# Attention times FFN on one core: sums spread through DRAM, weights transposed on TensorE, another order beside the output products

## The chip, the cores and the metric

The kernel runs on one core of a Trainium2 chip. The metric is device time in microseconds (us) of one execution, the median of several. The engines are TensorE (PE, with its weight loads as PEld), VectorE (DVE), ScalarE (ACT), GpSimd (POOL) and SyncE (SP, which here only issues DMAs). Each engine runs its own instructions in the order in which the program gives them, and waits on semaphores for the others.

## The reference

The input x has 4 batches of 512 rows of 512 floats. Attention and a quantised FFN work on the same normalised x and are multiplied:

```python
xn = layernorm(x)
q, k, v = split(xn @ w_qkv)                 # 16 heads of 32
q, k = rope(rmsnorm(q) * q_gamma), rope(rmsnorm(k) * k_gamma)
s = softmax(causal(q @ k.T / sqrt(32))) @ v @ w_out
W = lambda wq, scale: (wq - 128) * scale[:, None]    # wq are int32
g = silu((silu(xn @ W(wq_gate).T) * (xn @ W(wq_up).T)) @ W(wq_down).T)
out = x + s * g
```

Gate and up weights are 1408 x 512, the down weights 512 x 1408, all as int32 with small values. The scales are applied after the products.

## The kernel before

One launch holds everything. The work is cut into 16 units: batch b (0 to 3) by head group g (0 to 3, four heads each). The order is written out by hand (a manual schedule): the program text's order is each engine's order, and there is no planner. Each unit is a hidden window followed by an attention window.

**The hidden window** (`hidden_window`, L702) computes FFN hidden tiles f of one chunk (chunks of 2, 3, 3, 3 tiles for g = 0 to 3; a tile is 256 of the gate and up rows). `hidden` (L578) makes the products (L585, x split into a high part xh and a rest xl in two f32r products), `gate` and `gated` (L594, L599) the silu and product. Between them stand fills: the last probabilities of the unit before, its sums, the transposes of the new q and k (`Projection.turn`, L417), in norm windows the transposes of the next batch's x (`Norm.turn`, L342).

**The attention window** comes in three forms. Units (0,0) to (0,2) use `attention_window` (L759): probabilities are transposed on PE (`turn`, L493). Units (0,3) to (3,2) use `placed_window` (L824): DVE transposes 32 x 32 blocks (`blocks`, L511, instruction L521), and four DMAs on SP place them (`spread`, L523). Unit (3,3) uses `last_window`. In each, step t (0 to 3) takes query tile t: `scores` (L445), `probabilities` (L462; DVE masks and takes the row's minimum at L473, ACT exponentiates at L483 and sums the row), `values` (L536). Beside them run the next unit's qkv projection: `product` (L366, PE), `square` (L379: ACT squares q and k, then copies v out, L381 and L382) and `rotate` (L384: DVE L402, L405, L409; POOL L410, L316, L317, L412), and the down products `contract` (L624, L632).

Three special places: in **norm windows** (b,3) with b below 3, `Norm.cut` (L349) splits the next batch's xnT, with a copy on ACT and a subtraction L353 on the engine named (two on POOL, two on DVE in placed windows). In **g = 0 windows** of batches 1 to 3, `beside(t)` runs `Result.project` (L673, products L678) and `finish` (L686) of the batch before. In others it does nothing.

**Sums.** ACT leaves the row sums of the softmax, one column per head and tile. `spread_sums` (L547) takes reciprocals on DVE (L553) and repeats each over 32 columns on POOL (L554). `turn_sums` (L559) transposes that on PE (four transposes, L563), ACT copies the result to rT (L564), and `divide` (L566) multiplies the values' bank by rT on DVE.

**Weights.** The FFN weights are prepared once, during batch 0. 34 tiles are loaded as int32 (22 of gate and up with four 128 x 128 blocks each, 12 of down with 4, 4 or 3). `turn_weights` (L250) casts a tile to bf16 on ACT (L256) and starts a transposing DMA on SP (L258); `finish_weights` (L261) subtracts 128 on DVE into the final f32r place and collects the largest value (L265). The prologue (L967) does the first four; then `weights()` (L278) runs after each f of a hidden window and each t of an attention window in batch 0, until all are done:

```python
        for _ in range(n):
            if turning and now[0] - turning[0][0] >= 2:
                finish_weights()
        load_weights(n)
```

**PSUM.** There are four pools: ps_a with four banks (scores, qkv, hidden and output products), ps_t with two (`bank_t`, L104: all transposes, some qkv products), and one each for the values and for the down products.

Of the kernel before, what the change touches and what calls it, by code (L numbers as in the profile page):

```python
# [21 lines left out]
P = 128  # L22
# [29 lines left out]
def interleaved(  # L52
# [40 lines left out]
    ps_t = ctx.enter_context(tc.tile_pool(name="ps_t", bufs=2, space=PSUM))  # L93
    ps_v = ctx.enter_context(tc.tile_pool(name="ps_v", bufs=1, space=PSUM))
    ps_d = ctx.enter_context(tc.tile_pool(name="ps_d", bufs=1, space=PSUM))
    ctx.enter_context(tc.manual_schedule())

    def work(name):
# [86 lines left out]
    def load_scales():  # L185
# [5 lines left out]
            at += n  # L191
        return srow, at

    sdown = const.tile([P, D], F32, name="sdown")

    def prepare_scales(srow, at):
        tp = bank_t("sps")
# [32 lines left out]
    todo = list(preparations())  # L230
    n_prep = len(todo)
    largest = const.tile([P, n_prep], F32, name="largest")
    loaded, turning, finished = [], [], set()

# [10 lines left out]
                nc.sync.dma_start(raw.bitcast(U32), src.bitcast(U32))  # L247
                loaded.append((now[0], room, raw, k, dst, name))

    def turn_weights():  # L250


        _, room, raw, k, dst, name = loaded.pop(0)
        halves_ = raw.bitcast(BF16)
        n = k * P
        nc.scalar.copy(halves_[:, :n], raw.bitcast(U32))  # L256
        turned = halves_[:, n:].rearrange("p (c r) -> p c r", r=P)
        nc.sync.dma_start(turned, halves_[:, :n], transpose=True)  # L258
        turning.append((now[0], room, turned, k, dst, name))

    def finish_weights():  # L261

        _, room, turned, k, dst, name = turning.pop(0)
        i = len(finished)
        nc.vector.tensor_scalar(  # L265
            dst,
            turned,
            -ZERO_POINT,
            None,
            ALU.add,  # L270
            ALU.max,
            accum_out=largest[:, i : i + 1],
        )
        if len(finished) >= NC:
            rooms.append(room)
        finished.add(name)

    def weights(n=2):  # L278

        now[0] += 1  # L280
        for _ in range(n):
            if turning and now[0] - turning[0][0] >= 2:
                finish_weights()
        load_weights(n)
        for _ in range(n):
            if loaded and now[0] - loaded[0][0] >= 1:
                turn_weights()

    def find_wide():

# [69 lines left out]
    class Projection:  # L360
# [16 lines left out]
            self.banks[t] = bank  # L377

        def square(self, t):  # L379
            bank = self.banks[t]  # L380
            nc.scalar.activation(squares, bank[:, : 2 * P], AF.Square)  # L381
            nc.scalar.copy(self.v[:, t, :], bank[:, 2 * P :])  # L382

        def rotate(self, t, squared=False):  # L384


            bank = self.banks[t]
            name = f"{self.b}_{self.g}_{t}"
            if not squared:
                self.square(t)  # L390
            qk = qp.tile([P, 2 * P], F32, tag="qk", name=f"qk_{name}")
            qs = tp_.tile([P, 2 * P], F32, tag="qs", name=f"qs_{name}")

            def four(a):
                return a.rearrange("p (i h d) -> p i h d", i=2, d=HD)

            def table(k, cols):
                a = tab[:, t, :, k, cols]
                return a.unsqueeze(2).to_broadcast([P, 2, HPG, a.shape[-1]])

            bank4 = four(bank[:, : 2 * P])
            nc.vector.tensor_tensor(four(qk), bank4, table(0, slice(0, HD)), ALU.mult)  # L402
            for lo, hi in ((0, half), (half, 0)):
                lo, hi = slice(lo, lo + half), slice(hi, hi + half)
                nc.vector.tensor_tensor(  # L405
                    four(qs)[:, :, :, lo], bank4[:, :, :, hi], table(1, lo), ALU.mult
                )
            ss = small.tile([P, 2 * HPG], F32, tag="ss", name=f"ss_{name}")
            nc.vector.tensor_reduce(ss, heads(squares), AX.X, ALU.add)  # L409
            nc.gpsimd.tensor_tensor(qk, qk, qs, ALU.add)  # L410
            inverse_root(ss, ss, HD * RMS_EPS)
            nc.gpsimd.tensor_tensor(  # L412
                heads(qk), heads(qk), ss.unsqueeze(2).to_broadcast([P, 2 * HPG, HD]), ALU.mult
            )
            self.qk[t] = qk
# [15 lines left out]
    class Step:  # L431
# [30 lines left out]
        def probabilities(self, *js):  # L462

            for j in js:
                if self.first is not None:
                    pr = piece(self.first, self.t + 1)[:, j * self.keys : (j + 1) * self.keys]
                else:
                    i = j % self.per
                    if i == 0:
                        self.pieces.append(next_piece("pr"))  # L470
                    pr = self.pieces[-1][:, i * self.keys : (i + 1) * self.keys]
                least = self.least[:, j : j + 1]
                nc.vector.tensor_tensor_reduce(  # L473
                    out=pr,
                    in0=self.banks[j],
                    in1=mask[:, N - self.keys :],
                    scale=float(HD),
                    scalar=3.0e38,
                    op0=ALU.add,
                    op1=ALU.min,  # L480
                    accum_out=least,
                )
                nc.scalar.activation(  # L483
                    pr,
                    pr,
                    AF.Exp,
                    bias=least,
                    scale=-1.0,
                    accum_out=self.sums[:, self.t, j : j + 1],
                )  # L490
                self.probs.append(pr)

# [54 lines left out]
        def spread_sums(self, tiles=range(NT)):  # L547

            n, cols = len(tiles), slice(tiles[0] * P, (tiles[-1] + 1) * P)
            if tiles[0] == 0:  # L550
                self.sums_spread, self.rT = work(f"spread_{self.id}"), work(f"rT_{self.id}")
            sums = self.sums[:, tiles[0] : tiles[0] + n, :]
            nc.vector.reciprocal(sums, sums)  # L553
            nc.gpsimd.tensor_copy(  # L554
                heads(self.sums_spread[:, cols]),
                sums.rearrange("p t j -> p (t j)").unsqueeze(2).to_broadcast([P, n * HPG, HD]),
            )

        def turn_sums(self, tiles=range(NT)):  # L559
            cols = slice(tiles[0] * P, (tiles[-1] + 1) * P)  # L560
# [5 lines left out]
        def divide(self, tiles=range(NT)):  # L566
# [2 lines left out]
                oT[:, self.g, cols], self.pv[:, cols], self.rT[:, cols], ALU.mult  # L569
            )  # L570

    def steps(b, g, v):
        sums = small.tile([P, NT, HPG], F32, tag="sums", name=f"sums_{b}_{g}")
        pv = ps_v.tile([P, N], F32, tag="pv", name=f"pv_{b}_{g}")
        return [Step(b, g, t, v, sums, pv) for t in range(NT)]

# [125 lines left out]
    def hidden_window(b, g, last, fresh, result, norm, beside):  # L702

        placed = last is not None and last.placed
        if result is not None and not placed:
            result.gate(0)

# [5 lines left out]
        def turned(*tiles):  # L715
# [4 lines left out]
        fills = [  # L720
            lambda: drain(0),
            lambda: drain(2),
            lambda: (last.spread_sums(), fresh.turn()) if last is not None else None,
            lambda: turned(0, 1),
            lambda: turned(2),
            lambda: turned(3),
# [1 line left out]
        for i, f in enumerate(chunks[g]):  # L728
# [22 lines left out]
                fresh.turn()  # L751
            if b == 0:
                weights()
        if last is not None:
            last.turn_sums()
            if not placed:
                last.values()
# [66 lines left out]
    def placed_window(b, g, last, s, fresh, norm, result):  # L824

        def halves(engine, *tiles):
            if norm is not None:
                for t in tiles:  # L830
                    norm.cut(t, engine)

        def beside(t):
            if result is not None:
# [8 lines left out]
        def values():  # L843
            for t in range(NT - 1):
                s[t].values()

        load(0)
        s[0].scores()
        s[1].scores(s[0].whole, s[0].keys)
# [4 lines left out]
        adds = contract_two(b, g)  # L854
        s[1].probabilities(0, 1, 2, 3)
        adds[0]()
        if g == 0:
            fresh.rotate(0, squared=True)
        if last.placed:
            last.values()  # L860
        s[2].scores()
        adds[1]()
        if g == 0:
            last.divide()
        s[0].blocks(0, 1, 2, 3)
        s[0].spread()
        s[2].probabilities(0, 1, 2, 3)
        add = contract(b, g, 2)
        s[2].blocks(0, 1, 2, 3)
        s[2].spread()  # L870
        if g:
            fresh.product(0)
            fresh.rotate(0)
        s[1].blocks(0, 1, 2, 3)
        s[1].spread()
        load(1, 2)
        if g == 0:
            add()
        halves(nc.gpsimd, 0, 1)
        for t in range(NT):  # L880
            if t:

                fresh.product(t, other=t == NT - 1 or (g > 0 and t == NT - 2))
                fresh.rotate(t)
            if t == 1 and g:
                add()
                last.divide()
            if t == 1:
                halves(nc.vector, 2, 3)
            beside(t)  # L890
            if t == 1:
                load(3)
# [74 lines left out]
    def prologue():  # L967
# [18 lines left out]
        norm.cut(3, nc.vector)  # L986
        load_weights(3)
        for _ in range(4):
            turn_weights()
        fresh.product(1)  # L990
        fresh.rotate(1)
        for _ in range(4):
            turn_weights()
        for t in range(2, NT):
            fresh.product(t)
            fresh.rotate(t)
            finish_weights()
            finish_weights()
        load_wqkv(slice(1, 2))
        now[0] += 1  # L1000
        prepare_scales(*scales_in)
# [3 lines left out]
    for u, (b, g) in enumerate(units):  # L1005
# [17 lines left out]
                done.store(t)  # L1023
        if (b, g) == (0, NC - 1):
            next(finding)
            nc.sync.dma_start(wout, w_out.rearrange("(c p) m -> p c m", p=P))
        if b == 0 and 2 + g < NC:
            load_wqkv(slice(2 + g, 3 + g))
        if (b, g) == (0, 0):
            nc.sync.dma_start(sdown, s_down.partition_broadcast(P))  # L1030
        if (b, g) == (0, NC - 2):
            finding = find_wide()
            next(finding)
# [485 lines left out]
```

## Time and profile before

| what | before |
|---|---|
| median of 3 executions | 659.25 us (658.75 to 659.99) |
| profiled execution | 656.71 us |
| its span | 654.9 us (1.8 us lie around it) |
| PE busy | 622.2 us, 95% of the span |
| DVE busy | 482.4 us, 74% |
| ACT busy | 346.3 us, 53% |
| POOL busy | 317.0 us, 48% |
| mean granted TensorE clock | 0.992 |
| DMA | 62.63 MB in 65584 packets |

The profiled execution is 2.5 us below the median. Busy shares are averages over very different stages: batch 0 carries the weights, batches 1 to 3 the output products of the batch before. The profile's chain of work follows the last instruction back to what released it; the waits add up idle time by what ended it; the timeline gives start, duration, engine, line and operation of merged instructions, with idle time and releaser in brackets; and the windows view gives busy time and the granted clock in chosen stretches.

### The profile page before, as it was taken

To read this page: it belongs to the slowest core of one execution; us is meant where nothing else is said; L and a number is where in the kernel's file an instruction comes from. 1 tells how busy PE (TensorE), PEld (TensorE's weight loads), DVE (VectorE), ACT (ScalarE), POOL (GpSimd) and SP (SyncE) were. 2 spreads that over 40 slices of the span, in tenths; PEclk is the share of its full clock that TensorE was granted. 3 is DMA by queue.
4 is the path that set the end of the run, shared out by engine and by line. 5 is a ranking of instruction groups with operands and counts; after the bars stand their busy time and mean duration, and the time that the engine had idled before them with its cause. 6 is when DMAs were issued, how large, how long until landed. Compare 5 with 4: busy or idle time off the path is not lost.

```text
span 654.9 us, 11673 instructions
## 1 busy us (share of the span) xinstructions
PE 622.2 (95%) x3906; PEld 413.7 (63%) x3906; DVE 482.4 (74%) x1248; ACT 346.3 (53%) x895; POOL 317.0 (48%) x365
## 2 busy tenths in 40 slices
PE   4989999999988999999998999999997999999995
PEld 3646757667564576758664476767765467676752
DVE  4677776755988479797998369799798657969553
ACT  2666765646473264546755046464756136464560
POOL 3925235352563626544382633637194442727422
PEclk9999999999999999999998999999999899999999
DMA  8594853100433146243323425523233505333401
GB/s 267 144 215 110 185 133 101 66 1 1 98 82 87 59 130 162 66 96 66 79 44 81 121 48 144 137 61 83 65 80 82 145 1 146 82 73 89 130 1 70
DMA packets 65584, 62.63 MB, mean 96 GB/s; under 512 B 22998, under 2 KB 48876, under 8 KB 65516
## 3 DMA queue, kind: packets, MB, share of 16 engines
q1 hardware_dynamic: 64556, 61.38, 37.7%
q8 instruction: 33, 0.54, 0.3%
q10 hardware_dynamic: 960, 0.43, 0.2%
q14 instruction: 35, 0.29, 0.1%
HBM read 21.80 MB, written 4.19 MB: 40 GB/s over the span
## 4 chain that ended last, share of the span: by engine, by line
PE 79%; DVE 12%; ACT 4%; issue 2%; DMA 2%; POOL 0%; DVEq 0%; ACTq 0%
PE h L585 22%; PE qkv L370 21%; PE so L678 9%; PE sc L452 5%; PE dn L632 5%; PE dn L615 5%; PE pv L539 5%; DVE arena L521 3%; PE pt L499 2%; DVE arena L473 2%; PE qkt L422 2%; DVE qs L405 1%; PE rt L563 1%; ACT arena L483 1%; PE xnt L346 1%
## 5 line engine op out<-in xcount | busy, mean ns | idle before, releaser
L370 PE MATMUL qkv<-wqkv,xnT 128*128 128x384 f32 x512 | 172.5, 490 | 2.3 <-DVE least L473 2.3
L483 ACT ACTIVATE arena<-arena,least 128x128 f32<-128x128 f32 (+3 forms) x256 | 140.6, 551 | 63.4 <-DVE least L473 63.2
L370 PEld LDWEIGHTS qkv<-wqkv,xnT 128*128 128x128 f32 x512 | 96.3, 191 | 69.0 <-issue 4.2
L521 DVE STREAM_TRANSPOSE arena<-arena 128x512 f32<-128x512 f32 (+1 forms) x132 | 126.1, 1002 | 0.0
L410 POOL TENSOR_TENSOR qk<-qk,qs 128x256 f32<-128x256 f32 x64 | 48.2, 753 | 156.0 <-DVE qs L405 156.0
L473 DVE CUSTOM_DVE_ANT_0 arena<-sc,mask 128x128 f32<-128x128 f32 (+3 forms) x256 | 109.3, 485 | 15.1 <-PE sc L452 13.8
L604 POOL TENSOR_TENSOR h<-sil,h 128x512 fp32r<-128x512 f32 x44 | 57.9, 1315 | 110.5 <-ACT h L603 110.5
L317 POOL TENSOR_TENSOR ss<-ss,minus_half 128x8 f32<-128x8 f32 x64 | 106.9, 1671 | 5.3
L381 ACT ACTIVATE squares<-qkv 128x256 f32<-128x256 f32 x64 | 24.5, 383 | 122.5 <-PE qkv L370 98.0
L602 DVE SCALAR_TENSOR_TENSOR sil<-h,scales,sil 128x512 f32<-128x512 f32 x44 | 32.7, 743 | 52.6 <-PE h L585 43.7
L678 PE MATMUL so<-wout,oT 128*128 128x512 f32 x128 | 61.9, 625 | 6.6 <-DVE least L473 6.6
L603 ACT CAST h<-sil 128x512 fp32r<-128x512 f32 x44 | 27.3, 620 | 72.3 <-DVE sil L602 72.3
L402 DVE TENSOR_TENSOR qk<-qkv,tab 128x256 f32<-128x256 f32 x64 | 26.4, 412 | 44.7 <-ACT v L382 44.3
L632 PE MATMUL dn<-wdT,h 128*128 128x512 f32 x208 | 59.0, 419 | 0.0
L632 PEld LDWEIGHTS dn<-wdT,h 128*128 128x128 f32 x208 | 36.9, 188 | 25.8 <-issue 16.0
L585 PE MATMUL h<-xh,wuT 128*128 128x512 f32 x176 | 50.0, 406 | 1.7 <-ACT qT L125 1.7
L585 PE MATMUL h<-xh,wgT 128*128 128x512 f32 x176 | 50.0, 406 | 0.7 <-ACT v L382 0.7
L452 PE MATMUL sc<-kT,qT 32*128 32x512 f32 (+3 forms) x512 | 48.8, 467 | 1.4 <-DVE wdT L265 1.4
L585 PE MATMUL h<-xl,wgT 128*128 128x512 f32 x176 | 48.2, 395 | 0.0
L585 PE MATMUL h<-xl,wuT 128*128 128x512 f32 x176 | 48.1, 395 | 0.0
L483 ACT ACTIVATION_READ_ACCUMULATOR arena<-arena,least 128x1 f32 x256 | 47.9, 187 | 0.0
L678 PEld LDWEIGHTS so<-wout,oT 128*128 128x128 f32 x128 | 24.7, 199 | 33.9 <-issue 23.6
(92 smaller groups left out, 920.7 us busy)
## 6 DMA issues: line engine op xcount, KB each, us to landing
arena<-arena SPq DMA_DIRECT2D x48, 256.0 KB, 4.8
arena<-arena SPq DMA_DIRECT2D x48, 192.0 KB, 3.6
arena<-arena SPq DMA_DIRECT2D x48, 128.0 KB, 3.2
x<-in_L_attn_x SPq DMA_DIRECT2D x16, 256.0 KB, 4.3
out<-o SPq DMA_DIRECT2D x15, 256.0 KB, 4.4
wqkv<-in_L_attn_w_qkv SPq DMA_DIRECT2D x16, 192.0 KB, 3.4
arena<-arena SPq DMA_DIRECT2D x48, 64.0 KB, 2.1
xr<-in_L_attn_x SPq DMA_DIRECT2D x12, 256.0 KB, 3.8
```

What stands on the lines that cost most here:

```text
L317: nc.gpsimd.tensor_tensor(dst, dst, minus_half[:, : dst.shape[-1]], ALU.pow)
L370: nc.tensor.matmul(bank.rearrange("p (i d) -> p i d", i=3), lhsT=xnT[:, c, ts(t, P)], rhs=wqkv[:, c, :, self.g, :], start=(c == 0), stop=( ...
L410: nc.gpsimd.tensor_tensor(qk, qk, qs, ALU.add)
L452: nc.tensor.matmul(bank, lhsT=qT[rows, ts(self.t, P)], rhs=kT[rows, : self.keys], start=True, stop=True,)
L473: nc.vector.tensor_tensor_reduce(out=pr, in0=self.banks[j], in1=mask[:, N - self.keys :], scale=float(HD), scalar=3.0e38, op0=ALU.add, op1 ...
L483: nc.scalar.activation(pr, pr, AF.Exp, bias=least, scale=-1.0, accum_out=self.sums[:, self.t, j : j + 1],)
L521: nc.vector.transpose(way[:, :, blocks], probs[:, :, blocks])
L539: nc.tensor.matmul(self.pv[j * HD : (j + 1) * HD, ts(self.t, P)], lhsT=self.v[:, k, ts(j, HD)], rhs=self.turned[j][:, k], start=(k == 0), ...
L585: nc.tensor.matmul(bank, lhsT=w[:, c, ts(f, P)], rhs=a[:, c, :], start=(c == 0 and a is xh), stop=(c == NC - 1 and a is xl),)
L604: nc.gpsimd.tensor_tensor(to[:, 1, :], sil, to[:, 0, :].bitcast(F32), ALU.subtract)
L632: nc.tensor.matmul(bank, lhsT=h[:, i, a, ts(t, P)], rhs=wdT[:, f, :], start=(i == 0 and a == 0), stop=(f == fs[-1] and a == 1),)
L678: nc.tensor.matmul(self.banks[t], lhsT=oT[:, g, ts(t, P)], rhs=wout[:, g, :], start=(g == 0), stop=(g == NC - 1),)
```

## The change

The change has three parts.

1. **Sums.** In the hidden windows of (b,g) with b above 0 and g above 0, but not (3,3) (8 of 16 units, called `far`), the sums of the unit before are no longer repeated on POOL and transposed on PE. `send_sums` takes the reciprocal and one 32 x 32 block transpose on DVE and writes the result to a DRAM tile with four DMAs; `receive_sums`, called in the placed window between the spreads, reads it back with four DMAs that each broadcast a row to 32 partitions. All sums live in one constant tile.
2. **Weights.** The transposing DMAs go. `cast_weights` casts (one step later than before), and `turn_weights` transposes two tiles on PE into one bank of ps_t, with DVE's subtraction reading PSUM. The identity in bf16 lies in the tile of the down scales, whose load moves to unit (0,3).
3. **Order in `placed_window`.** With g = 0 the next unit's first rotation (and v's copy, now apart from the squares) and s0's blocks and spread come after s2's probabilities. In norm windows all cuts come first and all subtractions go to POOL, the last rotation's addition goes to DVE, and s0's blocks come after s2's probabilities.

```diff
-    def turn_weights():
+    def cast_weights():
...
-        halves_ = raw.bitcast(BF16)
-        n = k * P
-        nc.scalar.copy(halves_[:, :n], raw.bitcast(U32))
-        turned = halves_[:, n:].rearrange("p (c r) -> p c r", r=P)
-        nc.sync.dma_start(turned, halves_[:, :n], transpose=True)
...
+        narrow = raw.bitcast(BF16)[:, : k * P]
+        nc.scalar.copy(narrow, raw.bitcast(U32))
+        cast.append((now[0], room, narrow, k, dst, name))
+
+    def turn_weights(n=2):
+        bank = bank_t(f"wt_{len(finished)}").bitcast(BF16)
+        for i in range(n):
+            _, room, narrow, k, dst, name = cast.pop(0)
+            turned = bank[:, i * 4 * P : (i * 4 + k) * P]
+            for c in range(k):
+                nc.tensor.transpose(turned[:, ts(c, P)], narrow[:, ts(c, P)], ident16)
+            at = len(finished)
+            nc.vector.tensor_scalar(
+                dst,
+                turned.rearrange("p (c r) -> p c r", r=P),
...
     def weights(n=2):
         now[0] += 1
-        for _ in range(n):
-            if turning and now[0] - turning[0][0] >= 2:
-                finish_weights()
+        ready = [c for c in cast[:n] if now[0] - c[0] >= 1]
+        if ready:
+            turn_weights(len(ready))
         load_weights(n)
         for _ in range(n):
-            if loaded and now[0] - loaded[0][0] >= 1:
-                turn_weights()
+            if loaded and now[0] - loaded[0][0] >= 2:
+                cast_weights()
...
+        def send_sums(self):
+            sums = self.sums[:, :HPG, :]
+            nc.vector.reciprocal(sums, sums)
+            nc.vector.transpose(sums_turned, self.sums.rearrange("p j t -> p (j t)"))
+            self.rows = dram.tile([HPG * NT, 4, 32], F32, tag="sums", name=f"rows_{self.id}")
+            for q in range(4):
+                nc.sync.dma_start(self.rows[:, q, :], sums_turned[q * 32 : q * 32 + HPG * NT, :])
+
+        def receive_sums(self):
+            self.rT = work(f"rT_{self.id}")
+            for j in range(HPG):
+                nc.sync.dma_start(
+                    self.rT[j * HD : (j + 1) * HD, :],
+                    self.rows[ts(j, NT), :, :].rearrange("t q s -> (t q s)").partition_broadcast(HD),
+                )
...
     # hidden_window
+        far = placed and g > 0 and (b, g) != units[-1]
...
-            lambda: (last.spread_sums(), fresh.turn()) if last is not None else None,
+            lambda: (last.send_sums() if far else last.spread_sums(), fresh.turn()) if last is not None else None,
...
-        if last is not None:
+        if last is not None and not far:
             last.turn_sums()
...
     # placed_window
+        if norm is not None:
+            for t in range(NT):
+                norm.cut(t)
         load(0)
...
         adds[0]()
-        if g == 0:
-            fresh.rotate(0, squared=True)
...
         if g == 0:
             last.divide()
-        s[0].blocks(0, 1, 2, 3)
-        s[0].spread()
+        elif norm is None:
+            blocks(0)
         s[2].probabilities(0, 1, 2, 3)
         add = contract(b, g, 2)
-        s[2].blocks(0, 1, 2, 3)
-        s[2].spread()
-        if g:
+        if g == 0:
+            blocks(0)
+            fresh.rotate(0, squared=True)
+            fresh.keep(0)
+            blocks(2, 1)
+            add()
+        else:
+            if norm is not None:
+                blocks(0)
+            if last.placed:
+                last.receive_sums()
+            blocks(2)
             fresh.product(0)
             fresh.rotate(0)
-        s[1].blocks(0, 1, 2, 3)
-        s[1].spread()
+            blocks(1)
         load(1, 2)
-        if g == 0:
-            add()
-        halves(nc.gpsimd, 0, 1)
         for t in range(NT):
             if t:
                 fresh.product(t, other=t == NT - 1 or (g > 0 and t == NT - 2))
-                fresh.rotate(t)
+                fresh.rotate(t, adder=nc.vector if norm is not None and t == NT - 1 else nc.gpsimd)
...
-            if t == 1:
-                halves(nc.vector, 2, 3)
...
     def prologue():
...
         for t in range(2, NT):
             fresh.product(t)
             fresh.rotate(t)
-            finish_weights()
-            finish_weights()
+            turn_weights()
```

## The prediction

> **What bounds the kernel now.** I read the page first: engines, clock row, chain.
>
> ```profile
> PE 622.2 (95%) x3906; PEld 413.7 (63%) x3906; DVE 482.4 (74%) x1248; ACT 346.3 (53%) x895; POOL 317.0 (48%) x365
> ...
> PEclk9999999999999999999998999999999899999999
> ...
> PE 79%; DVE 12%; ACT 4%; issue 2%; DMA 2%; POOL 0%; DVEq 0%; ACTq 0%
> ```
>
> TensorE (PE) is busy for 95% of the span and carries 79% of the chain, and it is busy in the opening stages too (slices 2 to 10 show 8 or 9 tenths). So what keeps PE waiting lengthens the kernel, and work taken off PE shortens it. Two slices have a lower clock. Next the waits, first of PE, then of VectorE (DVE): total us, times, longest.
>
> ```profile
> PE so L678 <- DVE least L473: 6.6, 3, 2.2
> PE qkt L422 <- POOL qk L412: 2.6, 3, 1.3
> ...
> DVE qk L402 <- ACT v L382: 44.3, 32, 2.5
> ```
>
> The first row is the stall that the reordering aims at, in the windows with output products (g=0, batches 1 to 3). The last row matters for the weights: L402 reads the q and k columns of a PSUM bank, L382 copies the v columns of that bank, neither needs the other's result, and still one waits. The program orders engines by PSUM bank, not by columns.
>
> The timeline of one such stall, PE's row for the same place a batch earlier, and the windows view (PE's granted clock is the column before the DMA share):
>
> ```profile
> 350.19 1.20 PE L632 MATMUL dn<-wdT,h 128*128 128x512 f32 x4
> ...
> 352.03 1.07 DVE L521 STREAM_TRANSPOSE arena<-arena 128x512 f32<-128x512 f32 x1
> 353.02 0.52 DVE L473 CUSTOM_DVE_ANT_0 arena<-sc,mask 128x384 f32<-128x384 f32 x1
> 353.59 5.40 PE L678 MATMUL so<-wout,oT 128*128 128x512 f32 x8 [2.20 <-DVE least L473]
> ```
> ```profile
> 201.80 3.70 PE L678 MATMUL so<-wout,oT 128*128 128x512 f32 x8 [2.21 <-DVE least L473]
> ```
> ```profile
> 201.80:205.20 3.40, 3.40 (x8) 1.63 (x9) 3.40 (x9) 2.48 (x8) 0.52 (x1) 1.00 0.35 77
> 354.90:358.20 3.30, 3.30 (x5) 1.33 (x4) 3.30 (x7) 1.18 (x4) 0.00 (x0) 0.50 0.27 60
> ```
>
> PE runs dry at 351.39, because DVE rotates tile 0 and transposes s0's blocks before it reaches s2's masks, which free the bank. After two of the three such stalls (this one and that at 505) the granted clock was 0.50 for about 3.4 us, and the same eight products took 5.40 instead of 3.70: 1.7 us more. Last, a window of batch 0, where weights are prepared:
>
> ```profile
> 39.91 2.75 PE L370 MATMUL qkv<-wqkv,xnT 128*128 128x384 f32 x8
> 42.21 1.38 PE L632 MATMUL dn<-wdT,h 128*128 128x512 f32 x4
> 42.76 0.39 ACT L381 ACTIVATE squares<-qkv 128x256 f32<-128x256 f32 x1 [1.10 <-PE qkv L370]
> 43.04 0.26 ACT L382 COPY v<-qkv 128x128 f32<-128x128 f32 x1
> 43.34 0.42 DVE L402 TENSOR_TENSOR qk<-qkv,tab 128x256 f32<-128x256 f32 x1 [1.93 <-ACT v L382]
> 44.07 0.41 DVE L409 TENSOR_REDUCE ss<-squares 128x8 f32<-128x256 f32 x1
> 44.40 0.68 DVE L265 TENSOR_SCALAR_CACHE_REDUCE wgT<-oT 128x512 fp32r<-128x512 bf16 x1
> ```
>
> PE goes from the qkv product straight to the down products, 0.3 us before ACT even squares. The weights come by DMA; nothing on PE waits for them here.
>
> **The weights, the large term.** Removed: 34 DMA transposes (SP and queue time; PE waits for none). Added: 132 PE transposes, in 17 blocks of two tiles. The nearest rows for one: four f32r products of 512 columns at L585 follow each other every 0.93 (25.62, 26.55, 27.48), 0.058 for 128 columns; the eight fp32 transposes of L422 at 32.15 take 1.03, the last alone 0.27, so 0.109 apart. That is 7.7 to 14.4 us, if they only pass; between two like widths I take 0.075, 10 us.
>
> They do not only pass. One bank holds both tiles, and the loop issues tile 0's four transposes, tile 0's tensor_scalar on DVE, and then tile 1's transposes into the same bank. By the L402 row and by the order in which the changed program is built, tile 1's first transpose waits for tile 0's tensor_scalar, in each of the 17 blocks. PE is in order, so all behind it stands, and on DVE that tensor_scalar stands behind the rotation. Replayed with the rows above: PE ends the qkv product at about 42.5 and tile 0 soon after, then waits for ACT (42.76 to 43.3), the rotation (43.34 to 44.4) and tensor_scalar (44.40 to 45.08); with tile 1's 0.3 it is free at 45.4 instead of 42.5. A block here costs 2.9 us, 2.3 of it idle. In a hidden window the wait is for the silu product (L602, 0.75) and tensor_scalar 0.68, with both tiles' transposes: 2.0. Stage by stage:
> - prologue (2 blocks): before, the first gate product starts at 24.62. Now product(3) waits for rotation 2 (v copied at 22.70) and its tensor_scalar until 24.5, ends at 27.1, and the second block repeats copies 0.65, rotation 1.1, tensor_scalar 0.7 and tile 1, with latencies: about 30.6, +6.0.
> - hidden (0,0), 2 blocks: +2.9 with the waits that stay, but 2.0 come back, since the probabilities there waited for a cast that waited for a DMA (PE gaps of 1.36 and 1.06 at 33.2 and 37.5): +0.9.
> - attention (0,0): 2.9+2.9+2.8+2.0 = 10.6, less 1.8 of waits for DVE that lie there today (0.62, 0.75 and smaller): +8.8.
> - hidden (0,1): 3 x 2.0 = +6.0. Attention (0,1): 10.6 less 1.4: +9.2. Hidden (0,2): 2 x 1.9 = +3.8.
>
> Together +34.7, the transposes' 10 included. Bounds: +20 if DVE, running ahead in the stalls, gives back much of them later; +45 if nothing is absorbed.
>
> **The clock.** Two of three 2.2 us gaps led to half clock, 1.7 each. The change adds some ten gaps of 2 to 3 us; only some will fall as those two did. I take three periods, +5; bounds 0 and +10. The Trainium skill ("TensorE: Matmul & The Clock Gate", "HAM oscillation — how this bites in real kernels") states as its rule that no idle gap of PE should exceed about 3.4 us. By that rule gaps of 2.3 us cost no clock and this term would be 0; the 0.50 row behind a 2.20 gap speaks against it, and I go by the row.
>
> The skill's page "PSUM — Partial Sum Buffer" ("Summary: rules for kernel authors") says that whoever reads PSUM while matmuls run should use a different bank, and guard by bank. That speaks against two tiles in one bank; with a bank for each tile the block would cost its transposes and little else, the 10 us of the first rival below.
>
> **The order beside output products (g=0).** Rotation 0 (1.2) and s0's blocks (1.07) move behind s2's probabilities, so these start near 350.1 and not 353.0, and PE's next bank is free when it runs dry: 3 x 2.2 = 6.6, and the two half-clock periods 3.4: −10.0. The moved steps find cover under the output products (3.7). s0's SP transfers go with them; their readers come after the last beside(). Bounds −6.6 and −12.
>
> **The norm windows (b,3).** All cuts go to POOL (4 x 1.49), which frees two cuts of 1.25 on DVE; rotation 3's add goes from POOL to DVE. The window ends with the gap at qkt L422 (1.35, 0.65, 0.62 in three). POOL's last chain (3.4 us) starts earlier; I take 1.7 + 0.9 + 0.9: −3.5. Bounds 0 and −4.3. s1's spread, issued later on SP, lands near 331.5 where the values start at 330.7; that is in the lower bound.
>
> **The sums.** In 8 of 16 units four rt transposes leave PE (0.5 us in a row), ACT's copy (0.58) and POOL's spread (0.7) hide anyway. In six units PE gains 0.5, in the two norm ones 0.15, because scores there wait for DVE: −3.3. Bounds 0 and −4.2. Added: DVE 0.3, SP 8 issues of 0.6 each. The four receiving ones queue on SP between s0's and s2's spread, where SP idles 2.54 us (401.5 to 404.1), 2.4 us of issue; the divide comes 5 us later. So I cost them at nothing; uncovered they push s2's and s1's spread by 2.4.
>
> **Sum.** Profiled run 656.7 (span 654.9 and 1.8 around it): 656.7 + 34.7 + 5 − 10.0 − 3.5 − 3.3 = 679.6. The median before lies 2.5 above its profiled run: **682**.
>
> **Rivals.**
> 1. Faster, 652. The bank does not hold PE, or DVE is there in time, and the 132 transposes only pass. Then 659.25 + 10 − 16.8 = 652.5. It turns at 16.8 / 17 = 0.99 us a block. For it: DVE has 26% idle. Against: the wait stands in the built order, and the rotation ahead of it cannot start before ACT's copy. 0.10.
> 2. Still slower, 694: nothing absorbed (+45) and half clock more often than not (+7). For it: DVE is late in the attention windows already. 0.17.
> 3. The gains fail: receiving DMAs arrive late, the divide holds DVE ahead of the last probabilities, 1 us in 8 units, and the reordered g=0 windows find a new wait as long as half of the old: 682 + 8 + 5 = 695. For it: DMA landings of 2 to 5 us, two in a row. Against: the SP idle time. 0.10.
>
> **Numbers.** The forecast has 0.61; 0.02 is left for about break-even. What is within 0.2% (1.3 us), about what a measurement can tell from no change, is "same". Faster 0.10, same 0.02, slower 0.88. The forecast's own bounds (+20, clock 0, full gains: 664; +45, +10: 697) with rivals 2 and 3 give 664 to 698; outside lie rival 1 and the upper tail.
>
> **What would show it.** Right: PE waits at the new transposes for DVE's tensor_scalar, 17 times, some 30 us in all; the first gate product near 30; the 2.2 gaps at L678 gone, with them the half clock there, but half clock between 20 and 150 us; the time past batch 0 shorter by about 17. Wrong: no such waits in the list; then the time is near 652. A row of DVE's divide waiting for a DMA would show rival 3.

## The result, and the profile after

The changed kernel takes 687.4 us (median of 4 executions, 686.4 to 690.21) beside 659.0 for the kernel before on the same chip: ratio 1.0445, 95% interval 1.0398 to 1.0493. Its profiled execution took 686.40 us with a span of 684.6. The forecast was 682, its range 664 to 698.

The page of the changed kernel first: engines, granted clock, chain of work.

```profile
PE 631.3 (92%) x4006; PEld 419.3 (61%) x4006; DVE 482.1 (70%) x1253; ACT 342.4 (50%) x887; POOL 316.0 (46%) x362
...
PEclk9998999999999999999999999999999999999999
...
PE 81%; DVE 8%; ACT 6%; DMA 2%; issue 1%; SPq 1%; DVEq 0%; ACTq 0%
```

PE's busy time grew by 9 us only, the span by 30: PE now waits. The dip of the clock row has moved from late slices to an early one. PE's waits (total us, times, longest) say where; wt is the bank of the weight transposes, L269 the transposes, L271 DVE's subtraction:

```profile
PE wt L269 <- DVE wgT L271: 20.9, 10, 3.1
PE xnt L352 <- DVE x L344: 8.7, 3, 8.2
PE wt L269 <- DVE wdT L271: 6.4, 5, 2.8
PE wt L269 <- ACT h L633: 2.6, 2, 1.3
PE h L615 <- ACT qT L126: 2.1, 3, 0.9
PE pv L547 <- DMA arena<-arena: 1.7, 2, 1.1
```

The rows for so and qkt of before are gone. In their place stand 15 waits of the transposes for the subtraction, 27.3 us, two that show ACT as their last releaser, and a new one: the values (pv) wait for a DMA. The timeline of the window that the prediction replayed, now 9 us later:

```profile
51.68 0.39 PE L269 MATMUL wt<-sdown,oT 128*128 128x128 bf16 x4
52.26 0.38 ACT L386 ACTIVATE squares<-qkv 128x256 f32<-128x256 f32 x1 [1.43 <-PE wt L269]
52.53 0.26 ACT L389 COPY v<-qkv 128x128 f32<-128x128 f32 x1
...
52.83 0.42 DVE L410 TENSOR_TENSOR qk<-qkv,tab 128x256 f32<-128x256 f32 x1 [2.25 <-ACT v L389]
...
53.89 0.68 DVE L271 TENSOR_SCALAR_CACHE_REDUCE wgT<-wt 128x512 fp32r<-128x512 bf16 x1
...
54.63 0.58 PE L269 MATMUL wt<-sdown,oT 128*128 128x128 bf16 x4 [2.57 <-DVE wgT L271]
54.97 2.05 PE L662 MATMUL dn<-wdT,h 128*128 128x512 f32 x4
```

Four transposes, then nothing on PE for 2.57 us while ACT squares and copies, DVE rotates and subtracts; then the second tile's four. The four down products after it took 2.05 rather than 1.38: half clock, as the windows view shows (granted clock before the DMA share):

```profile
23.80:27.20 3.40, 2.78 (x8) 1.83 (x8) 1.26 (x4) 0.00 (x0) 3.23 (x5) 0.50 0.00 0
54.90:58.30 3.40, 3.40 (x23) 1.90 (x21) 1.39 (x3) 0.00 (x0) 2.19 (x2) 0.55 0.28 77
64.70:68.10 3.40, 3.38 (x28) 2.12 (x27) 1.39 (x3) 0.00 (x0) 2.40 (x3) 0.51 0.23 81
112.80:116.20 3.40, 3.40 (x18) 2.15 (x17) 1.01 (x3) 0.00 (x0) 2.25 (x2) 0.53 0.22 63
```

Last, the place of the old 2.2 us stall, a g=0 window:

```profile
388.46 1.20 PE L662 MATMUL dn<-wdT,h 128*128 128x512 f32 x4
389.50 3.60 PE L708 MATMUL so<-wout,oT 128*128 128x512 f32 x8
```

No idle time, and 3.60 for eight output products where it was 5.40.

**Where the time went.** How far the changed kernel lies behind the kernel before, from the two timelines. A unit ends at the first FFN product of the next one, a hidden window at the first score behind it:

| stage | delay at its end | change in it |
|---|---|---|
| prologue | +7.1 | +7.1 |
| unit (0,0) | +21.0 | +13.8 |
| unit (0,1) | +37.3 | +16.4 |
| hidden window (0,2) | +42.7 | +5.3 |
| norm windows (0,3), (1,3), (2,3), from their first down product to the next unit's first score | | −1.5, +0.1, +0.4 |
| g=0 windows (1,0), (2,0), (3,0) | | −2.5, −4.2, −4.3 |
| hidden windows with sums through DRAM, six without a norm | | 6 x −0.43 = −2.6 |
| the same, (1,3) and (2,3), up to their first down product | | 0.0, 0.0 |
| attention windows (1,2), (2,2) | | +0.3, +0.3 |
| behind the first score of (3,3) | | +0.7 |
| end of the span | +29.7 | |

In (1,3) and (2,3) the first score comes 0.43 and 0.46 us earlier too, but the 16 score products then take 0.43 longer than before, and the down products behind them gain nothing. First the kernel before, then the changed one, in (1,3):

```profile
310.29 1.03 PE L452 MATMUL sc<-kT,qT 32*128 32x128 f32 x16
```
```profile
348.06 1.46 PE L460 MATMUL sc<-kT,qT 32*128 32x128 f32 x16
```

The list of waits names nothing for this; e1, e5, e7 and e8 show the same 0.43 in the same two units.

### The profile page after: what moved, and what is told of

Its sections match the earlier page's. It is cut to its first block, busy times and chain, and to the rows that moved or that the text cites. A ratio compares the mean times of both kernels' runs of the same rounds, so it can differ in the third digit from the quotient of the medians.

```text
span 684.6 us, 11883 instructions
## 1 busy us (share of the span) xinstructions
PE 631.3 (92%) x4006; PEld 419.3 (61%) x4006; DVE 482.1 (70%) x1253; ACT 342.4 (50%) x887; POOL 316.0 (46%) x362
## 4 chain that ended last, share of the span: by engine, by line
PE 81%; DVE 8%; ACT 6%; DMA 2%; issue 1%; SPq 1%; DVEq 0%; ACTq 0%
PE h L615 23%; PE qkv L376 21%; PE so L708 8%; PE dn L662 7%; PE sc L460 6%; PE pv L547 5%; PE dn L645 5%; ACT arena L491 2%; PE pt L507 2%; PE qkt L430 2%; PE wt L269 1%; DVE sil L632 1%; DVE wgT L271 1%; DMA x<-in_L_attn_x 1%; DMA arena<-arena 1%
## 5 line engine op out<-in xcount | busy, mean ns | idle before, releaser
L418 POOL TENSOR_TENSOR qk<-qk,qs 128x256 f32<-128x256 f32 x61 | 44.6, 731 | 167.3 <-DVE qs L413 167.3
L633 ACT CAST h<-sil 128x512 fp32r<-128x512 f32 x44 | 27.3, 620 | 73.7 <-DVE sil L632 73.7
L662 PE MATMUL dn<-wdT,h 128*128 128x512 f32 x208 | 61.2, 431 | 0.0
L708 PE MATMUL so<-wout,oT 128*128 128x512 f32 x128 | 58.1, 593 | 0.0
L662 PEld LDWEIGHTS dn<-wdT,h 128*128 128x128 f32 x208 | 38.4, 198 | 25.2 <-issue 12.9
L460 PE MATMUL sc<-kT,qT 32*128 32x128 f32 (+3 forms) x512 | 49.3, 470 | 0.1
L547 PE MATMUL pv<-arena,v 128*32 128x128 f32 x1280 | 44.7, 279 | 1.8 <-DMA arena<-arena 1.7
```

Source lines behind the costliest of these rows:

```text
L418: adder.tensor_tensor(qk, qk, qs, ALU.add)
L460: nc.tensor.matmul(bank, lhsT=qT[rows, ts(self.t, P)], rhs=kT[rows, : self.keys], start=True, stop=True,)
L547: nc.tensor.matmul(self.pv[j * HD : (j + 1) * HD, ts(self.t, P)], lhsT=self.v[:, k, ts(j, HD)], rhs=self.turned[j][:, k], start=(k == 0), ...
L662: nc.tensor.matmul(bank, lhsT=h[:, i, a, ts(t, P)], rhs=wdT[:, f, :], start=(i == 0 and a == 0), stop=(f == fs[-1] and a == 1),)
L708: nc.tensor.matmul(self.banks[t], lhsT=oT[:, g, ts(t, P)], rhs=wout[:, g, :], start=(g == 0), stop=(g == NC - 1),)
```

## The experiments

The first four ran together, beside 658.48 us of the kernel before; the others together, beside 658.98.

**e1: weights by DMA again.** The changed kernel with the functions of the weights as before.

```diff
-        nc.scalar.copy(narrow, raw.bitcast(U32))
-        cast.append((now[0], room, narrow, k, dst, name))
+        nc.scalar.copy(halves_[:, :n], raw.bitcast(U32))
+        turned = halves_[:, n:].rearrange("p (c r) -> p c r", r=P)
+        nc.sync.dma_start(turned, halves_[:, :n], transpose=True)
+        turning.append((now[0], room, turned, k, dst, name))
```

> The changed kernel with the weights' part undone: tiles are transposed by DMAs again, sums and order stay changed. Theory (stalls of TensorE inside the weight blocks and the half clock behind them cost all of the loss): by the milestones of the two traces batch 0 lost 42.7 us up to the first product of unit (0,3), and everything later gained 13 net, so this kernel takes 687.4 - 42.7 = 645 us (642 to 648), faster than the kernel before by about 2%. Rival A (the loss comes from the parts together, for example the moved load of the down scales or the DRAM sums disturbing the start): between 650 and 680. Rival B (the later gains need the delayed start): about 659.

Measured 644.48 us (644.14 to 644.88), ratio 0.978 (0.974 to 0.9821). The delay at unit (0,3) is 0.3 us instead of 42.7, and the later gains stay. So the weights' part costs 42.9 us, and the rest of the change gains 14.0. Both rivals fall.

**e2: both tiles' transposes first.** Same bank, same instructions, another order.

```diff
         for i in range(n):
...
             for c in range(k):
                 nc.tensor.transpose(turned[:, ts(c, P)], narrow[:, ts(c, P)], ident16)
+            both.append((room, turned, dst, name))
+        for room, turned, dst, name in both:
             at = len(finished)
             nc.vector.tensor_scalar(
```

> The changed kernel, with one edit: both tiles' transposes are issued before the two subtractions on VectorE, still in one bank. Nothing else differs, the number of transposes is the same. Theory (the wait inside a block, for VectorE's subtraction of the first tile, is the cost): TensorE's waits at the weight transposes for that subtraction (27.3 us in the trace) go, the four half-clock periods of batch 0 (about 1.6 each) mostly go, some 4 to 6 us of waits that batch 0 had before come back, so 655 to 662 us. Rival A (the 132 transposes themselves, or bank pressure in the pool of two banks, are the cost): 675 to 687.

Measured 653.69 us (651.83 to 654.35), ratio 0.9917 (0.988 to 0.9953): 33.7 us less than the changed kernel, a little more than the theory gave. The same window in its timeline:

```profile
44.04 0.61 PE L269 MATMUL wt<-sdown,oT 128*128 128x128 bf16 x8
44.46 1.17 PE L664 MATMUL dn<-wdT,h 128*128 128x512 f32 x4
44.62 0.38 ACT L388 ACTIVATE squares<-qkv 128x256 f32<-128x256 f32 x1 [1.42 <-PE wt L269]
```

Eight transposes in 0.61, and the down products follow at once, before ACT has squared. PE's list has no wait of wt for the subtraction any more, and the windows of batch 0 show no half clock. (One period of it stands in unit (2,3), behind a wait of the values for a DMA of 1.9 us.) At unit (0,3) the delay is 8.0 us for 132 transposes, 0.061 each, net of the waits that came and went. The first product of unit (0,0) comes 1.1 and 1.5 us later in e5 and e6, whose edits do not touch what stands ahead of it, so the 8.0 is no sharper than that.

**e3: a bank for each tile.** The text's order stays as in the changed kernel.

```diff
-        bank = bank_t(f"wt_{len(finished)}").bitcast(BF16)
         for i in range(n):
+            bank = bank_t(f"wt_{len(finished)}").bitcast(BF16)
             _, room, narrow, k, dst, name = cast.pop(0)
-            turned = bank[:, i * 4 * P : (i * 4 + k) * P]
+            turned = bank[:, : k * P]
```

> The changed kernel, with a bank of the two-bank pool for each tile instead of one bank for two tiles; the order of the program text is unchanged (transposes, subtraction, transposes, subtraction). Theory (sharing one bank makes the second tile wait): the second tile's transposes no longer wait for the first tile's subtraction, so most of the 27.3 us of waits goes, as when the transposes are issued first; but both banks are taken, so that a user of either before or behind a block may wait: 655 to 668 us. Rival A (it is bank pressure, not the wait inside the block): no better than now, 687, or slower. Rival B (TensorE waits for VectorE for another reason, such as the cast tiles): 685 to 690.

Measured 656.05 us (655.23 to 657.89), ratio 0.9954 (0.9936 to 0.9972). The wait inside the block is gone here too but for 0.5 us, so it came from the shared bank. The median is 2.4 us above e2, the delay at unit (0,3) is 12.0 instead of 8.0. Its list of PE's waits shows other users that wait for the two banks, which fits; no run shows that they are all of it:

```profile
PE sps L202 <- DVE wgT L271: 1.3, 1, 1.3
PE rt L588 <- DVE wgT L271: 1.1, 1, 1.1
```

**e4: the weights' part alone.** The kernel before with the weights' functions of the changed kernel (the diff of the change's second part and nothing else).

> The kernel before, with the weights' part of the change alone (cast a step later, transposes on TensorE, two tiles in one bank, down scales loaded later). Theory: the loss of batch 0 stands by itself: 659.0 + 42.7 = 702 us (697 to 706). Rival (parts interact): under 690.

Measured 702.32 us (698.61 to 704.09), ratio 1.065 (1.0592 to 1.0709): 43.8 us, as by the milestones. Its delay at unit (0,3) is 43.1. The parts add up.

**e5: the sums' part alone.** The kernel before with the first part of the change.

```diff
+        if g and last.placed:
+            last.receive_sums()
         s[2].blocks(0, 1, 2, 3)
         s[2].spread()
```

> The kernel before, with the sums' part alone (eight units send the reciprocal sums through DRAM; received between s0's and s2's spread). Theory: each of the eight hidden windows ends 0.43 us earlier, as in the changed kernel, -3.5 together; in the two norm windows that receive sums, the four receiving issues push s1's spread on SP by about 2.4 us, past the start of the values, which costs 0.5 to 1 each: 656 us beside 658.5 (655 to 657). Rival (the divide waits for the DMAs): 659 or more.

Measured 656.24 us (654.4 to 658.42), ratio 0.9952 (0.9925 to 0.9979). The number came out, the reason given for it did not. Seven of the eight hidden windows end 0.42 to 0.46 us earlier, that of (2,3) 0.25. The two norm windows that receive sums take 0.4 and 0.5 us longer from their first score on, but that is the 0.43 of the score products above: from the first down product on they change by −0.03 and +0.03. Neither the values nor the divide wait for a DMA here, so the receiving issues cost nothing as long as the order of the norm windows stays.

**e6: the g=0 order alone.** The kernel before with the third part's g=0 branch.

```diff
         adds[0]()
-        if g == 0:
-            fresh.rotate(0, squared=True)
...
         s[2].probabilities(0, 1, 2, 3)
         add = contract(b, g, 2)
+        if g == 0:
+            s[0].blocks(0, 1, 2, 3)
+            s[0].spread()
+            fresh.rotate(0, squared=True)
+            fresh.keep(0)
```

> The kernel before, with the reordering of the three g=0 windows alone. Theory: the 2.2 us stall before the first output products goes in each of three windows (6.6), and with it the two half-clock periods behind it (3.4): about -10 to -11, 648 us (647 to 650) beside 658.5. Rival (half clock has another cause): the stall goes, the half clock stays: 652. Rival (the moved rotation is the next stall): 654 or more.

Measured 648.9 us (646.53 to 649.11), ratio 0.9828 (0.98 to 0.9856): −10.1. By the timelines the three windows gain 2.5, 4.2 and 4.0; the first had no half clock in the profile of before, the other two had. The stall at L678 is gone from its list, and no half clock is left behind it. One period of half clock stands elsewhere, at 190.6 in the hidden window of (1,0), which is 1.5 us longer for it than in the profile of before.

**e7: the receiving DMAs early.** e1 with one edit in the norm windows.

```diff
         if norm is not None:
+            if last.placed:
+                last.receive_sums()
             for t in range(NT):
                 norm.cut(t)
...
-            if last.placed:
+            if last.placed and norm is None:
                 last.receive_sums()
```

> The kernel with weights transposed by DMA (644.5), with one edit: in the two norm windows that receive sums, the four receiving DMAs are issued at the window's start, where SP idles, and not between the spreads. Theory (they push s1's spread on SP, and the values wait for it): TensorE's wait for that DMA (1.9 us in two windows) goes, 642.6 us (642 to 643.5). Rival (the spread is late because VectorE transposes s1's blocks late, whatever SP does): 644 to 645, with the wait still in the list.

Measured 641.78 us (641.23 to 643.71), ratio 0.9734 (0.9711 to 0.9757), the fastest kernel here, 0.2 below the range. The same place in e1 and then in e7 (SP's issues, the values):

```profile
318.61 1.85 SPq L575 DMA_DIRECT2D rT<-rows  x4
320.57 5.97 SPq L534 DMA_DIRECT2D arena<-arena  x8
...
328.76 1.30 PE L543 MATMUL pv<-arena,v 128*32 128x128 f32 x40 [1.00 <-DMA arena<-arena]
```
```profile
316.56 9.28 SPq L534 DMA_DIRECT2D arena<-arena  x12
...
327.95 1.52 PE L543 MATMUL pv<-arena,v 128*32 128x128 f32 x48
```

With the receiving issues out of the way the twelve spreads (s0, s2, s1) follow one another with no other issue between them, and the values run in one piece. The two windows are 1.1 and 1.2 us shorter than in e1. One wait of the values for a DMA (0.7 us) shows instead in unit (2,2), a window that the edit does not touch; it is there in e8 too (0.4), and its cause stays open. The profiled execution of e7 is its slowest.

**e8: the norm windows' order undone.** e7 with the old order there.

```diff
-        if norm is not None:
...
-            for t in range(NT):
-                norm.cut(t)
...
+        halves(nc.gpsimd, 0, 1)
...
-                fresh.rotate(t, adder=nc.vector if norm is not None and t == NT - 1 else nc.gpsimd)
+                fresh.rotate(t)
...
+            if t == 1:
+                halves(nc.vector, 2, 3)
```

> As the kernel before in this list (receiving DMAs at the start of the norm windows, weights by DMA), and the norm windows' order undone: two cuts on POOL and two on VectorE after the first rotations, the last addition on POOL, s0's blocks ahead of s2's probabilities. Theory (the norm order by itself shortens the window, by 1.0 to 1.5 each, the late spread took it back): 3 to 4 us slower than with it, 645.5 to 647, and TensorE's wait for POOL at the q/k transposes (2.6 us in three windows) is back. Rival (the norm order brings nothing): 642 to 643.5, as with it.

Measured 646.35 us (644.13 to 646.91), ratio 0.9795 (0.9771 to 0.9819), 4.6 above e7. The wait at the q/k transposes is back:

```profile
PE qkt L426 <- POOL qk L416: 2.8, 3, 1.3
```

By the timelines the three norm windows are 0.8, 0.8 and 1.1 longer than in e7, 2.7 together; where the rest of the 4.6 lies is not shown (the two profiled executions are 1.7 apart). So the norm order does gain what the forecast gave it, short of 0.8, where SP's queue does not take it back.

## Why the prediction was right, and where it was off

- **The wait inside the block** (the main term) is shown by e2 and e3: one edit of order, or one of banks, takes 33.7 or 31.4 us away without one instruction less on PE. The replay held: the second four transposes start 2.57 us after PE went idle, against 2.3. The rival that the bank does not hold PE is what e2 builds, and there it came out at 653.7 against its price of 652.5.
- **The transposes themselves** cost 0.061 each (e2), not 0.075: 8.0 instead of 10. The spacing agrees with the f32r row, not with a value between the rows: in e2 eight in 0.61, of which the last takes 0.22, is 0.056 apart.
- **Weights and clock together** were put at 34.7 + 5 = 39.7; the delay at unit (0,3) is 42.7. Four half-clock periods came instead of three (one in the prologue, +7.1 for +6.0). At 1.6 each, an estimate from 2.05 for 1.38 us of down products and the length of a period (in e4, e5 and e6 one period makes the hidden window of (1,0) 1.5 to 1.6 longer), they make 6.4; with 8.0 for the transposes, 28.3 are left for the stalls, where the forecast's 34.7 held 24.7. So what the stalls would absorb or give back was taken too large, by some 3.6, and the transposes' price too high by 2. By stages it lies in two hidden windows: (0,0) took +2.9 instead of +0.9, as the 2.0 that were to come back did not come back there, and (0,2) +5.3 instead of +3.8.
- **The clock.** The Trainium skill ("TensorE: Matmul & The Clock Gate", "HAM oscillation — how this bites in real kernels") gives about 3.4 us of idle time as the point to stay below. Here PE gaps of 3.14, 2.57, 2.25 and 2.19 us were each followed by half clock (others of 2.24, 2.25 and 2.79 were not), so weighing the row and not the rule was right: by the rule the term was 0. In e1, e3, e7 and e8, whose longest PE gap after the start is 1.4 us, no half clock is granted before PE's last product. But e6, with no longer gap, has one period: the length of a single gap is not what decides (last section).
- **The bank.** The skill's "PSUM — Partial Sum Buffer" ("Summary: rules for kernel authors") asks for another bank when PSUM is read beside matmuls. e3 gives each tile its own; e2 keeps one bank for two tiles, but PE is done with it and at work in another (dn) when DVE reads, and e2 is the faster: what counts here is that PE isn't made to wait for a reader in the middle of a block.
- **The g=0 order:** −10.0 forecast, −10.9 in the traces, −10.1 alone (e6). **The sums:** −3.3 forecast, −2.0 in the traces. The six other units gave 0.43 each, where 0.5 was forecast. The two norm units gave nothing, where 0.15 was forecast, since their scores give back what the transposes leave; the forecast had the place right. That its reason, a wait for DVE, is the right one is not shown. The windows of (1,2) and (2,2) lost 0.3 each, here and in e5; the reason stays open.
- **The norm windows** are the step that failed: −3.5 forecast, −1.0 measured, −1.5 + 0.1 + 0.4. The first, which receives no sums, gained; in the other two the values wait for s1's spread (0.68 and 1.06 us). The prediction had costed the receiving DMAs at nothing, with SP's idle 2.54 us of the kernel before as cover. e5 shows that the cover holds in the old order. But the change itself moves s0's blocks in norm windows, so the receiving issues and the three spreads stand in one queue behind each other, and the prediction had put the late spread into a bound rather than the sum. e7 takes the four issues out, the wait goes, and the three windows gain 0.9, 0.8 and 0.9. In this place the third rival was half right: not the divide, but the values behind the same queue.
- **Total:** 682 against 687.4. The profiled execution was put at 679.6 and took 686.4. Of these 6.8 us, 3.0 are weights and clock, 2.5 the norm windows, 1.3 the sums, and 0.7 lie behind the last unit's first score; the g=0 order gave 0.9 more than forecast. The time past batch 0 became shorter by 13.0 and not by about 17. The median lies only 1.0 above its profiled execution, where the forecast added 2.5; that it came 1.4 us nearer by this is luck.
- **Two slips** on which nothing rests: the forecast's lower bound adds up to 662 (682 less 14.7 and 5) and not to 664, and in the replayed window the down products start 0.55 us, not 0.3, ahead of ACT's squares (42.21 and 42.76).

## What to carry to other kernels

Where an in-order engine is the bound, read a new loop for what it makes that engine wait for in its middle: one bank for two tiles, with the reader's instruction between their writes, cost 34 us where the writes alone cost 8. Write all pieces first and let the reader follow, or leave work that the bounding engine need not do where it is hidden: no wait of PE in the kernel before names the DMA transposes, and they came out 8 us ahead of the best that PE did. And when DMAs are added to a queue, look for their cover in the order that the change will leave, in every window in which they are issued: here the idle time was there until another part of the same change used it up.

## What the runs showed of the hardware

Half clock follows much shorter idle times than expected, and not every time. In the sums' experiment (e5) PE idles 1.35 us and, 0.8 us later, 0.56, and the granted clock behind that is 0.50; in the profile of before, gaps of 1.35 and 0.55 at the same place leave it at full speed. The traces show what differs. In all ten, every change of the granted clock falls on a grid of 3.41 us (to within 0.02), which lies differently in each run, and what goes with half clock is PE's idle time within one stretch of the grid. Here are the two stretches of e5 and the two of before (length, then PE's busy time; granted clock before the DMA share):

```profile
186.56:189.98 3.42, 1.51 (x10) 1.03 (x9) 3.34 (x6) 1.99 (x4) 3.00 (x4) 1.00 0.00 0
189.98:193.39 3.41, 3.41 (x10) 2.52 (x10) 1.54 (x2) 1.26 (x2) 1.00 (x1) 0.50 0.84 123
```
```profile
184.19:187.60 3.41, 2.06 (x13) 1.54 (x12) 3.41 (x4) 2.27 (x4) 2.91 (x5) 1.00 0.00 0
187.60:191.01 3.41, 2.86 (x16) 2.05 (x14) 2.87 (x6) 2.14 (x4) 2.17 (x2) 1.00 0.55 90
```

In e5 both gaps lie in one stretch, 1.91 us idle; in before the grid cuts between them, 1.35 and 0.55. Between the first full clock (at 13.5 to 16.5 us) and PE's last product the ten traces have 19 stretches with 1.87 us of idle time or more, and 18 are followed by a stretch at half clock (the other, in e4, has 1.92); of those with 1.84 or less none is. It also sorts the stalls above: the gaps of 2.24, 2.25 and 2.79 us in the changed kernel, and the first of the three 2.2 us stalls of before, were cut, and left at most 1.61, 1.84, 1.83 and 1.66 us in one stretch. No run moved a gap against the grid, so this is a reading of ten traces and not an experiment.

The same instructions thus lose 1.6 us or not at the same place. In the kernel before this fits the spread: of its 24 executions beside the experiments the three fastest (656.13 to 656.6) have the highest mean clocks (0.992 and 0.993), the three slowest (661.15 to 661.89) the lowest (0.983 and 0.984). It does not explain all spread: in e7, whose profile has no half clock before PE's last product, executions of 641.36 and 643.71 us have the same mean clock of 0.999.
